# A two-layer metaformer on one Trainium2 core: image columns turned during the softmax, per-batch token scales, a pinned first norm

## The chip, the cores and the metric

The kernel runs on one core of a Trainium2 chip. The metric is the device time of one execution in microseconds (us); three executions are given by their median. Beside them stands one profiled execution, in which the hardware recorded every instruction of each engine. The engines are TensorE (PE in the profile; its weight loads are PEld), VectorE (DVE), ScalarE (ACT) and GpSimd (POOL); SyncE (SP) starts transfers. Each engine works through its own list of instructions and waits on semaphores for what others produce. On-chip data lies in SBUF (128 partitions) or, for results of TensorE, in PSUM.

## What is computed

The input is 4 batches of 32 images ("tokens") of 128 x 128 values. Layer 0 normalises each image row, runs an attention over tokens whose keys, queries and values come from Fourier convolutions, adds a mixer, and then a recurrent layer (FFN); layer 1 is an up/down convolution and a second FFN. The change touches the attention alone:

```python
tokens_norm = instance_norm(tokens, norm1_g, norm1_b)
k = fno_layer(tokens_norm, key_w, key_skip_w, key_skip_b, (Hs, Ws))
q = fno_layer(tokens_norm, query_w, query_skip_w, query_skip_b, (Hs, Ws))
v = fno_layer(tokens_norm, value_w, value_skip_w, value_skip_b, (H, W))
...
dprod = jax.nn.softmax(jnp.einsum('bhtd,bhsd->bhts', qf, kf) / scale, axis=-1)
attn = jnp.einsum('bhts,bhsd->bhtd', dprod, vf)
attn = fno_layer(attn, proj_w, proj_skip_w, proj_skip_b, (H, W))
attn = instance_norm(attn + tokens, attn_norm_g, attn_norm_b)
```

`x` reaches this part after a row norm: `x + _L0_conv_ref(_ln_c(x), ...)`. A convolution in `fno_layer` is a sum of a Fourier part over few frequencies and of a skip, a multiple of the image itself. So a score of head h between tokens t and s is a sum of a spectral product and of a multiple of the inner product ("gram") of the two images. The instance norm of a token is a factor s(t) on its image, and a score carries s(t) s(s).

## The kernel before

All images stay in SBUF as `XA[row, batch, token, column]`. The attention works in this order.

*Head.* `load` brings the images in eight rows of eight tokens for two batches first, with two loads of constants between them on SyncE's queue: L513 the first part, L519 the second (`cst[:, C_SW:]`). `stats(k, n)` (L737) takes for half batch k (16 images) the row statistics (`bn_stats`, one per image), a reciprocal root through `rsqrt_of` (L293 to L302: add, ACT root, reciprocal, four VectorE operations with a Newton step) and the factors r and nmr; `normalise(k, images)` (L759) applies them, 10 of 16 images on ScalarE (L765) and 6 on VectorE (L767). Two halves' statistics are written down first.

*Transforms.* The loop at L883 runs `transform(k)` over eight half batches: 16 images against 130 Fourier columns in groups of three (`ps_st1`, L782), copies to `A1` (L784 VectorE, L786 ScalarE), then the second Fourier dimension into `ps_pf` (L793) and the reduced images into `ps_pr` (L802), which ScalarE copies to `Rn` (L804). Between the groups, generators of other work are stepped: the statistics of the next batch, the weights' preparation (`weights`, which holds `ndcm`, L632), and `scores(b)` of the batch before.

*Scores* (L807). The coefficients `Frep` of a batch are gathered (`ps_fr`, L818), copied to `FK` (L825), multiplied with the query and key weights into `KM` (L832 to L847), transposed through `ps_kt` (L854), copied to `KT` by ScalarE (L855), and multiplied into the score tile `psc` (L858). `grams(k)` (L864) forms the inner products of the images of two batches from `Rn`.

*Softmax* (L899 to L967). After the loop the four scales `s4` come from `ps_s4`; the last batch's scores and the second grams follow. `Pm` is weight x gram + psc, times `sTL` (the product of the two tokens' scales), then max, subtraction, exponential, sum, reciprocal. The attention matrix is transposed (`ps_pt`, L949) and copied to `PTs` (L950) and its negative (L952); a weighted sum over heads gives `C`, which is transposed and spread over the blocks of `CTbd` (L967).

*Mixing.* `mix()` (L977) applies `CTbd` to all images at once. A chunk k is four image columns: four transposes bring (batch, token) to the partitions (`pt`, L982), ScalarE copies to `uT` (L984), four products give `pm` (L987), ScalarE copies them back to `XA` (L989) and squares them (L991, L994), and VectorE sums the squares (L995). Twenty of the chunks are interleaved with the Fourier part of the projection: 32 `df` products on VectorE (L1222) and bursts of `ps_y` on TensorE (L1235), one `mix` step after two or three of each four `df`.

The source order is not the order of execution. A scheduler places instructions by priorities from the source order and by their dependencies, on each engine apart, except where `in_order()` (L433) chains the instructions of each engine in a block to source order. Pools decide when buffers come free: `psa` holds two PSUM tiles (tag `st1`), `psb` three that `big(...)` hands out, and the mixing's PSUM pool `psm` takes over that space when these end.

Of the kernel before, what the change touches and what calls it, by code (L numbers as in the profile page):

```python
# [26 lines left out]
F32 = mybir.dt.float32  # L27
AF = mybir.ActivationFunctionType
ALU = mybir.AluOpType
# [3 lines left out]
P = 128  # L33
NB, NT = 4, 32
# [174 lines left out]
def _network(  # L209
# [53 lines left out]
    def scalar(name):  # L263
        o = len(HEAD_VECTORS) * NH + SCALARS.index(name)
        return sc[:, o : o + 1]
# [5 lines left out]
    def per_head(v):  # L271
        return v.unsqueeze(2).broadcast_to([P, NH, NT])
# [205 lines left out]
    PTs = WXY[:, 11072:12096].rearrange("p (a b c) -> p a b c", b=4, c=P)  # L478
    gram = aw.tile([P, NT], F32, name="gram")
# [15 lines left out]
    def big(name):  # L495
        return psb.tile([P, 512], F32, tag="big", name=name)
# [233 lines left out]
    with (  # L730
# [38 lines left out]
        def transform(k):  # L769
# [6 lines left out]
            normalise(k, range(0, 3))  # L776
            for n, j in enumerate(range(0, HB, 3)):
                m = min(3, HB - j)
                normalise(k, range(j + 3, min(j + 6, HB)))
                p = psa.tile([P, 3, 130], F32, tag="st1", name="ps_st1")  # L780
                for i in range(m):
                    mm(p[:, i, :], XA[:, b, t0 + j + i, :], cst[:, C_E : C_E + 130], start=True, stop=True)  # L782
                if n % 3 == 0:
                    nc.vector.tensor_copy(A1[:, j : j + m, :], p[:, :m])  # L784
                else:
                    nc.scalar.copy(A1[:, j : j + m, :], p[:, :m])  # L786
                yield True
# [19 lines left out]
        def scores(b):  # L807

            FF = sp.tile([P, 2, 16, NT], F32, tag="KM", name="FF")
# [4 lines left out]
            for g in range(4):  # L814
# [6 lines left out]
                if g % 2 == 1:  # L821
# [3 lines left out]
            nc.vector.tensor_copy(FK.rearrange("p r (k j w) -> p r k j w", k=8, j=2),  # L825
                                  Frep[:, b, :, :, 1:3, :WQ].rearrange("p k r j w -> p r k j w"))
# [49 lines left out]
        for k in range(2):  # L876
            for _ in stats(k, 1):
                pass
            if k == 0:
                next(prepare)  # L880
# [28 lines left out]
        for _ in before:  # L909
            pass  # L910

# [23 lines left out]
        Pm = sp.tile([P, NH, NT], F32, tag="KM", name="Pm")  # L935
        tt(Pm, per_head(wqk), per_token(gram), ALU.mult)
        tt(Pm, Pm, psc, ALU.add)
        tt(Pm, Pm, per_token(sTL), ALU.mult)
# [6 lines left out]
        tt(Pm, Pm, per_head(mx), ALU.mult)  # L945

        p = big("ps_pt").rearrange("p (g n) -> p g n", g=4)
        for g in range(4):
            nc.tensor.transpose(p[:, g], Pm[:, 4 * g : 4 * g + 4, :].rearrange("p h s -> p (h s)"), ident)  # L949
        tt(PTs[:, 0].rearrange("p g (b t) -> p g b t", b=NB), p.rearrange("p g (b t) -> p g b t", b=NB),  # L950
           s4.unsqueeze(1).unsqueeze(3).broadcast_to([P, 4, NB, NT]), ALU.mult)
        nc.scalar.mul(PTs[:, 1], PTs[:, 0], -1.0)  # L952

# [3 lines left out]
        Pv = sp.tile([P, NH, NT], F32, tag="KT", name="Pv")  # L957
        tt(Pv, Pm, per_head(pv_), ALU.mult)
        C = sp.tile([P, NT], F32, name="C")
        nc.vector.tensor_reduce(C, Pv.rearrange("p h s -> p s h"), AX.X, ALU.add)  # L960
        CT = sp.tile([P, NT], F32, name="CT")
        tt(C, C, sL, ALU.mult)
        tt(C, C, cst[:, C_ID : C_ID + 32], ALU.add)
        nc.vector.transpose(CT, C)
        for b in range(NB):
            q = slice(32 * b, 32 * b + 32)
            nc.vector.tensor_copy(CTbd[q, 32 * b : 32 * b + 32], CT[q])  # L967
# [9 lines left out]
    def mix():  # L977

        for k, w0 in enumerate(range(0, 80, 4)):
            pt = psm.tile([P, 4, P], F32, tag="pt", name="pt")  # L980
            for i in range(4):
                nc.tensor.transpose(pt[:, i, :], XA[:, :, :, w0 + i].rearrange("p b t -> p (b t)"), ident)  # L982
            uT = mp.tile([P, 4, P], F32, name="uT")
            nc.scalar.copy(uT, pt)  # L984
            pm = psm.tile([P, 4, P], F32, name="pm")
            for i in range(4):
                mm(pm[:, i, :], uT[:, i, :], CTbd, start=True, stop=True)  # L987
# [1208 lines left out]
```

## Time and profile before

| | us |
|---|---|
| median of three runs | 1044.66 |
| lowest and highest | 1043.44 and 1045.15 |
| profiled execution | 1045.66 |
| its span, first to last instruction | 1043.9 |

The mean granted clock of TensorE was 0.954 of full speed. Places in time are given from the start of the span. Operations that the change touches, in the profiled execution:

| operation | start, us | duration, us |
|---|---|---|
| first image norm on ScalarE, L765 | 17.80 | 3.19 for 8 |
| second constants load issued, L519 | 9.1 | 3.12 for the issue |
| `rep4` from those constants, POOL L524 | 16.8 | 0.32 |
| `FK` copy, batch 0, L825 | 43.23 | 0.31 |
| first `ps_kt` transposes, batch 0, L854 | 47.77 | 0.60 for 4 |
| `ps_s4` products, L901 | 112.53 | 1.05 for 4 |
| `psc` of the last batch, last four records, L858 | 123.81 | 1.90 |
| table load and first exponential, L912 | 123.34 | 1.28 |
| exponential of the scores, L942 | 128.80 | 0.63 |
| first `uT` copy, L984 | 134.83 | 0.59 |
| first `pm` products, L987 | 135.48 | 3.78 for two chunks |

How to read the lines below: a group names line, engine, operation, the tile written and the tile read, the shape and a count; TensorE's count of f32 products is two for each. In a timeline the bracket gives the engine's idle time before the group and the instruction that ended it. A chain of waits lists start, length and what ran, each piece released by the one before. The granted clock is the share of full speed that TensorE had.

### The profile page before, as it was taken

What the parts mean: (1) busy time and instruction counts of PE and PEld (TensorE: products, weight loads), DVE (VectorE), ACT (ScalarE), POOL (GpSimd) and SP (SyncE); (2) the same over time, 40 slices, a digit from 0 to 9 for tenths busy, and PEclk for the clock granted to TensorE, in tenths of its full rate; (3) what the DMA queues carried; (4) which work ended last, traced back from release to release, by engine and by line L of the source; (5) the groups of instructions that cost most, each with busy time, mean ns of one, the idle gap of its engine ahead of it and who ended that gap; (6) DMA issues with size and microseconds to landing.
All of it is one profiled execution on the core that took longest, in us unless ns stands there. A gap on an engine that the chain in (4) does not pass through costs nothing.

```text
span 1043.9 us, 18132 instructions
## 1 busy us (share of the span) xinstructions
PE 944.6 (90%) x6424; PEld 682.9 (65%) x6424; DVE 774.3 (74%) x2501; ACT 666.3 (64%) x1606; POOL 173.1 (17%) x298
## 2 busy tenths in 40 slices
PE   3999799977888999887998999999999999998995
PEld 2565466774655556534885777777777777776884
DVE  5986487775699998988888566665666666466997
ACT  3757356765567997967884545564656565556874
POOL 1000000021454436441001111102020202000000
PEclk9999989978789998999998999999999999999998
DMA  9723000001011110200000001000000000104543
GB/s 235 175 37 75 1 1 1 1 1 42 21 42 43 41 49 15 81 21 1 1 1 1 21 21 31 21 21 21 22 21 21 21 21 22 30 21 156 219 163 134
DMA packets 68965, 48.83 MB, mean 47 GB/s; under 512 B 4417, under 2 KB 63809, under 8 KB 68801
## 3 DMA queue, kind: packets, MB, share of 16 engines
q1 hardware_dynamic: 68529, 47.31, 15.7%
q8 instruction: 53, 0.87, 0.4%
q0 software_dynamic: 288, 0.01, 0.2%
q10 hardware_dynamic: 48, 0.26, 0.1%
q14 instruction: 47, 0.39, 0.1%
HBM read 30.68 MB, written 16.88 MB: 46 GB/s over the span
## 4 chain that ended last, share of the span: by engine, by line
PE 47%; DVE 24%; ACT 9%; POOL 6%; issue 3%; POOLq 0%; ACTq 0%; DVEq 0%
PE ps_scan L1841 8%; PE ps_up L1984 7%; PE ps_dn L1996 6%; PE ps_dn L2005 3%; PE ps_up L1973 3%; DVE XA L1511 3%; PE ps_wx L378 3%; PE ps_y L1235 2%; DVE XA L1510 2%; POOL c_r L292 2%; PE pm L987 2%; DVE U L1987 2%; POOL f_r L292 2%; PE ps_st L1353 2%; PE ps_inv L413 2%
## 5 line engine op out<-in xcount | busy, mean ns | idle before, releaser
L1987 DVE SCALAR_TENSOR_TENSOR U<-ps_up,above 128x512 f32<-128x512 f32 x128 | 86.7, 690 | 89.1 <-ACT above L1986 89.1
L1984 PE MATMUL ps_up<-q,WXY 128*128 128x512 f32 x256 | 123.6, 605 | 6.5 <-ACT q L1976 6.5
L1996 PEld LDWEIGHTS ps_dn<-WXY,U 128*128 128x128 f32 x1024 | 124.4, 192 | 3.3
L1996 PE MATMUL ps_dn<-WXY,U 128*128 128x128 f32 x1024 | 124.6, 275 | 0.0
L1842 DVE SCALAR_TENSOR_TENSOR ps_scan<-WXY,bs,ps_scan 128x128 f32<-128x128 f32 x352 | 103.6, 359 | 10.2 <-PE ps_scan L1841 7.3
L1986 ACT ACTIVATE above<-ps_up 128x512 f32<-128x512 f32 x128 | 74.3, 596 | 25.2 <-PE ps_up L1984 25.2
L1998 ACT COPY q<-ps_dn 128x512 f32<-128x512 f32 x64 | 37.5, 586 | 71.8 <-PE ps_dn L1996 71.8
L378 PE MATMUL ps_wx<-xt,wvt 128*128 128x512 f32 x128 | 68.8, 623 | 6.4 <-ACT WXY L385 4.2
L1973 PEld LDWEIGHTS ps_up<-WXY,XN 128*128 128x128 f32 x256 | 49.2, 192 | 34.5 <-issue 15.6
L292 POOL TENSOR_TENSOR f_r<-rs_e,neg_half 128x16 f32<-128x16 f32 (+2 forms) x10 | 23.9, 2394 | 278.6 <-DVE rs_e L291 244.1
L1984 PEld LDWEIGHTS ps_up<-q,WXY 128*128 128x128 f32 x256 | 44.0, 193 | 39.6 <-issue 23.9
L1973 PE MATMUL ps_up<-WXY,XN 128*128 128x256 f32 x256 | 66.8, 384 | 0.5 <-DVE XN L1943 0.5
L2005 PE MATMUL ps_dn<-q,WXY 128*128 128x256 f32 x256 | 66.0, 380 | 0.0
L1347 ACT ACTIVATE Z<-Z,k,aB 128x128 f32<-128x128 f32 x128 | 51.2, 482 | 11.7 <-DVE Z L1342 11.6
L2005 PEld LDWEIGHTS ps_dn<-q,WXY 128*128 128x128 f32 x256 | 46.1, 190 | 16.4 <-issue 12.0
L782 PE MATMUL ps_st<-cst,XA 128*128 128x130 f32 x256 | 43.3, 308 | 14.4 <-ACT XA L765 11.2
L385 ACT COPY WXY<-ps_wx 128x512 f32<-128x512 f32 x60 | 34.9, 582 | 28.6 <-DVE bn L381 28.4
L782 PEld LDWEIGHTS ps_st<-cst,XA 128*128 128x128 f32 x256 | 35.0, 204 | 27.5 <-ACT XA L765 12.4
L1568 ACT ACTIVATE xn<-XA,f_o,f_r 128x128 f32<-128x128 f32 x120 | 50.4, 487 | 2.7 <-DVE f_o L1550 2.2
L1945 ACT ACTIVATE XN<-XA,c_o,c_r 128x128 f32<-128x128 f32 x64 | 28.8, 490 | 31.8 <-DVE c_o L1934 25.9
L1511 DVE SCALAR_TENSOR_TENSOR XA<-Z,gB,XA 128x128 f32<-128x128 f32 x128 | 45.5, 355 | 4.7
L1510 DVE SCALAR_TENSOR_TENSOR XA<-ps_inv,r1B,xin 128x128 f32<-128x128 f32 x128 | 44.0, 344 | 6.4 <-PE ps_inv L1503 6.4
(436 smaller groups left out, 2147.4 us busy)
## 6 DMA issues: line engine op xcount, KB each, us to landing
XA<-in_x_dram SPq DMA_DIRECT2D x16, 512.0 KB, 7.3
xin<-in_x_dram SPq DMA_DIRECT2D x32, 256.0 KB, 3.2
turned<-XA SPq DMA_DIRECT2D x32, 256.0 KB, 2.3
XA<-turned SPq DMA_DIRECT2D x8, 1024.0 KB, 15.1
out_dram<-res SPq DMA_DIRECT2D x64, 128.0 KB, 2.1
WXY<-dd SPq DMA_DIRECT2D x4, 544.0 KB, 10.7
WXY<-md SPq DMA_DIRECT2D x4, 144.0 KB, 5.2
WXY<-m1d SPq DMA_DIRECT2D x1, 544.0 KB, 11.3
```

Source lines behind the costliest of these rows:

```text
L292: nc.gpsimd.tensor_tensor(o, e, neg_half[:, :n], ALU.pow)
L378: mm(self.held[t], self.t[:, 0, :], xt, start=True, stop=True)
L782: mm(p[:, i, :], XA[:, b, t0 + j + i, :], cst[:, C_E : C_E + 130], start=True, stop=True)
L1511: stt(a, Z[c][:, b, i], gB[c][:, n : n + 1], a, ALU.mult, ALU.add)
L1841: mm(p4, self.t[:, 1, :], prev, start=True, stop=True)
L1842: stt(p4, WX[:, :, h, :], s[:, 0:1], p4, ALU.mult, ALU.add)
L1973: mm(p[:, b, :], XN[u // 2][:, (u % 2) * H2 + b, :], UR.rearrange("p r q -> p (r q)"), start=True, stop=True)
L1984: mm(p, UC[:, s, :], q, start=True, stop=True)
L1986: nc.scalar.activation(above, p, AF.Relu, scale=1.0 - SLOPE)
L1987: stt(U[:, s], p, SLOPE, above, ALU.mult, ALU.add)
L1996: mm(p[:, r, b, :], U[:, s, b, r * P : (r + 1) * P], DC[:, s, :], start=(s == 0), stop=(s == 1))
L2005: mm(p, DR[:, r, :], q[:, r], start=(r == 0), stop=(r == 1))
```

## The change

Five things are done.

1. In the head the row statistics of half batch 0, the norm of all its 16 images and the statistics of half batch 1 are chained in this order by `in_order()`. `transform(0)` no longer norms.
2. The scale `s4` of a batch is computed at the start of its `scores(b)`. `FK` is multiplied by it on the way (two multiplies in place of one copy), so keys and queries both carry their own batch's scale. The gram part gets its scales by multiplying `gram` (128 x 32) with `sTL`, and the multiplication of `Pm` (128 x 512) goes.
3. `turn_images` transposes the columns of the first eight mixing chunks into `psa` tiles (`st1`, widened to 512 values) and ScalarE copies them to `turned_images`, a region of `WXY`. Four chunks stand in the source after the first product of `Pm`, four after the exponential.
4. `mix()` takes these eight chunks as they are and transposes only from chunk 8 on.
5. After the softmax's reciprocal a chained block computes `C` and `CTbd` first, from unnormalised `Pm` with the reciprocal in `pv_`, and then normalises, transposes and copies `PTs`.

```diff
@@ -476,6 +476,7 @@
+    turned_images = WXY[:, 12288:16384].rearrange("p (k i n) -> p k i n", k=8, i=4)
@@ -773,11 +774,13 @@
-            normalise(k, range(0, 3))
+            if k > 0:
+                normalise(k, range(0, 3))
             for n, j in enumerate(range(0, HB, 3)):
                 m = min(3, HB - j)
-                normalise(k, range(j + 3, min(j + 6, HB)))
-                p = psa.tile([P, 3, 130], F32, tag="st1", name="ps_st1")
+                if k > 0:
+                    normalise(k, range(j + 3, min(j + 6, HB)))
+                p = psa.tile([P, 512], F32, tag="st1", name="ps_st1")[:, : 3 * 130].rearrange("p (m n) -> p m n", m=3)
@@ -806,6 +809,12 @@
         def scores(b):
+            p = big("ps_s4")[:, :1]
+            mm(p, rv4[:, b].rearrange("p q t -> p (q t)"), mean_mat[:, 0:1], start=True, stop=True)
+            nc.vector.tensor_copy(s4[:, b : b + 1], p)
+            rsqrt_of(a1p, s4[:, b : b + 1], s4[:, b : b + 1], 1e-5, 1)
+            ts(s4[:, b : b + 1], s4[:, b : b + 1], scalar("norm1_g"), None, ALU.mult)
@@ -822,8 +831,9 @@
-            nc.vector.tensor_copy(FK.rearrange("p r (k j w) -> p r k j w", k=8, j=2),
-                                  Frep[:, b, :, :, 1:3, :WQ].rearrange("p k r j w -> p r k j w"))
+            for r in range(2):
+                ts(FK[:, r].rearrange("p (k j w) -> p k j w", k=8, j=2), Frep[:, b, :, r, 1:3, :WQ], s4[:, b : b + 1],
+                   None, ALU.mult)
@@ -873,11 +883,13 @@
-        for k in range(2):
-            for _ in stats(k, 1):
+        next(prepare)
+        with in_order():
+            for _ in stats(0, 1):
                 pass
-            if k == 0:
-                next(prepare)
+            normalise(0, range(HB))
+            for _ in stats(1, 1):
+                pass
@@ -894,20 +906,21 @@
-        p = big("ps_s4")[:, :NB]
-        for b in range(NB):
-            mm(p[:, b : b + 1], rv4[:, b].rearrange("p q t -> p (q t)"), mean_mat[:, 0:1], start=True, stop=True)
-        nc.vector.tensor_copy(s4, p)
-        rsqrt_of(a1p, s4, s4, 1e-5, NB)
-        ts(s4, s4, scalar("norm1_g"), None, ALU.mult)
         for _ in range(5):
             next(before)
         for _ in grams(1):
             pass
         for _ in before:
             pass
+        def turn_images(chunks):
+            for k in chunks:
+                p = psa.tile([P, 512], F32, tag="st1", name="ps_pt").rearrange("p (i n) -> p i n", i=4)
+                for i in range(4):
+                    nc.tensor.transpose(p[:, i, :], XA[:, :, :, 4 * k + i].rearrange("p b t -> p (b t)"), ident)
+                nc.scalar.copy(turned_images[:, k], p)
@@ -933,38 +946,41 @@
+        tt(gram, gram, sTL, ALU.mult)
         tt(Pm, per_head(wqk), per_token(gram), ALU.mult)
+        turn_images(range(0, 4))
         tt(Pm, Pm, psc, ALU.add)
-        tt(Pm, Pm, per_token(sTL), ALU.mult)
...
         nc.scalar.activation(Pm, Pm, AF.Exp)
+        turn_images(range(4, 8))
         nc.vector.tensor_reduce(mx, Pm, AX.X, ALU.add)
         nc.vector.reciprocal(mx, mx)
-        tt(Pm, Pm, per_head(mx), ALU.mult)
-
-        p = big("ps_pt").rearrange("p (g n) -> p g n", g=4)
...
-        tt(Pv, Pm, per_head(pv_), ALU.mult)
...
+        with in_order():
+            Pv = sp.tile([P, NH, NT], F32, tag="KT", name="Pv")
+            tt(pv_, pv_, mx, ALU.mult)
+            tt(Pv, Pm, per_head(pv_), ALU.mult)
+            C = sp.tile([P, NT], F32, name="C")
+            nc.vector.tensor_reduce(C, Pv.rearrange("p h s -> p s h"), AX.X, ALU.add)
...
+            for b in range(NB):
+                q = slice(32 * b, 32 * b + 32)
+                nc.vector.tensor_copy(CTbd[q, 32 * b : 32 * b + 32], CT[q])
+            tt(Pm, Pm, per_head(mx), ALU.mult)
+
+            p = big("ps_pt").rearrange("p (g n) -> p g n", g=4)
+            for g in range(4):
+                nc.tensor.transpose(p[:, g], Pm[:, 4 * g : 4 * g + 4, :].rearrange("p h s -> p (h s)"), ident)
...
+            nc.scalar.mul(PTs[:, 1], PTs[:, 0], -1.0)
@@ -977,11 +993,14 @@
         for k, w0 in enumerate(range(0, 80, 4)):
-            pt = psm.tile([P, 4, P], F32, tag="pt", name="pt")
...
+            if k < 8:
+                uT = turned_images[:, k]
+            else:
+                pt = psm.tile([P, 4, P], F32, tag="pt", name="pt")
...
```

More of the change, by code (lines that the diff above doesn't have):

```diff
@@ L942, in _network @@
         nc.scalar.activation(Pm, Pm, AF.Exp)
+        turn_images(range(4, 8))
         nc.vector.tensor_reduce(mx, Pm, AX.X, ALU.add)
         nc.vector.reciprocal(mx, mx)
-        tt(Pm, Pm, per_head(mx), ALU.mult)
-        p = big("ps_pt").rearrange("p (g n) -> p g n", g=4)
[L948 to L951, printed above, removed]
@@ L952, in _network @@
-        nc.scalar.mul(PTs[:, 1], PTs[:, 0], -1.0)
         pv_ = sp.tile([P, NH], F32, name="pv_")
         tt(pv_, head("proj_skip_w"), head("value_skip_w"), ALU.mult)
[L957 to L967, printed above, removed]
+        with in_order():
[4 more added lines that the diff above has]
+            nc.vector.tensor_reduce(C, Pv.rearrange("p h s -> p s h"), AX.X, ALU.add)
+            CT = sp.tile([P, NT], F32, name="CT")
+            tt(C, C, sL, ALU.mult)
+            tt(C, C, cst[:, C_ID : C_ID + 32], ALU.add)
+            nc.vector.transpose(CT, C)
+            for b in range(NB):
[5 more added lines that the diff above has]
+                nc.tensor.transpose(p[:, g], Pm[:, 4 * g : 4 * g + 4, :].rearrange("p h s -> p (h s)"), ident)
+            tt(PTs[:, 0].rearrange("p g (b t) -> p g b t", b=NB), p.rearrange("p g (b t) -> p g b t", b=NB),
+               s4.unsqueeze(1).unsqueeze(3).broadcast_to([P, 4, NB, NT]), ALU.mult)
+            nc.scalar.mul(PTs[:, 1], PTs[:, 0], -1.0)
@@ L979, in mix @@
         for k, w0 in enumerate(range(0, 80, 4)):
-            pt = psm.tile([P, 4, P], F32, tag="pt", name="pt")
[L981 to L984, printed above, removed]
+            if k < 8:
+                uT = turned_images[:, k]
+            else:
+                pt = psm.tile([P, 4, P], F32, tag="pt", name="pt")
+                for i in range(4):
+                    nc.tensor.transpose(pt[:, i, :], XA[:, :, :, w0 + i].rearrange("p b t -> p (b t)"), ident)
+                uT = mp.tile([P, 4, P], F32, name="uT")
+                nc.scalar.copy(uT, pt)
             pm = psm.tile([P, 4, P], F32, name="pm")
```

## The prediction

> **What bounds the kernel now.** I read the page first: busy shares (part 1) and the chain that ended last (part 4). TensorE is busy for 90% of the span and carries most of the chain, so time saved elsewhere counts only where TensorE waits for it.
>
> ```profile
> PE 944.6 (90%) x6424; PEld 682.9 (65%) x6424; DVE 774.3 (74%) x2501; ACT 666.3 (64%) x1606; POOL 173.1 (17%) x298
> ...
> PE 47%; DVE 24%; ACT 9%; POOL 6%; issue 3%; POOLq 0%; ACTq 0%; DVEq 0%
> ```
>
> All edits act before 205 us. I cut that stretch with the table of windows (us, then busy time and instruction count of PE, PEld, DVE, ACT, POOL, then granted clock, DMA share and GB/s): head, first scores, transforms, softmax, mixing.
>
> ```profile
> 0.00:48.00 48.00, 28.40 (x194) 20.26 (x195) 36.08 (x182) 26.06 (x67) 5.10 (x16) 1.00 0.95 222
> 48.00:63.00 15.00, 14.73 (x104) 8.23 (x102) 13.14 (x63) 9.35 (x23) 0.00 (x0) 1.00 0.02 6
> 63.00:113.00 50.00, 48.25 (x359) 29.72 (x357) 32.82 (x145) 30.11 (x72) 1.72 (x3) 1.00 0.29 57
> 113.00:133.50 20.50, 13.64 (x105) 9.58 (x104) 13.90 (x31) 6.79 (x17) 0.90 (x1) 0.81 0.00 1
> 133.50:204.20 70.70, 69.77 (x542) 46.95 (x542) 53.34 (x63) 45.58 (x72) 0.00 (x0) 0.96 0.00 1
> ```
>
> Mixing is TensorE's (69.8 of 70.7 us busy); the softmax is a chain with TensorE idle for 6.9 of 20.5 us. The head (DMA share 0.95) waits for data. The chain of waits through the softmax (start, us, what):
>
> ```profile
> 115.49 5.34 PE pg L868 x64
> 121.09 1.48 PE ps_kt L854 x12
> ...
> 123.88 1.85 PE psc L858 x4
> 125.75 0.69 DVE Pm L937
> 126.62 0.70 DVE Pm L938
> ...
> 130.47 0.70 DVE Pm L945
> 131.20 0.70 DVE Pv L958
> 131.92 1.01 DVE C L960
> 132.93 0.61 DVE WXY L950
> 133.59 2.00 PE pt L982 x8
> 135.59 3.67 PE pm L987 x16
> ```
>
> The timeline shows that TensorE's idle time is there, and which engine makes the head wait (duration, then idle before and releaser in brackets):
>
> ```profile
> 131.31 1.08 PE L949 MATMUL ps_pt<-ident,Pm 128*128 128x128 f32 x4 [5.59 <-DVE Pm L945]
> ```
>
> ```profile
> 121.77 1.56 ACT L855 COPY KT<-ps_kt 96x512 f32<-96x512 f32 x3
> ```
>
> [...] the three KT copies stand in one unbroken row in program order; so what the program now puts ahead of them delays them. [...] mean granted clock 0.54 from 130 to 140 us after the idle from 125.7, and two pm chunks (x16) take 3.67 us there where they take 2.2 us (2 x 1.10) later. [...]
>
> **The change, part by part.** The order in which the built program issues instructions on each engine, set against before's, decides here.
>
> *Head.* The first half batch's 16 norms now stand ahead of the 16 bn_stats of the second. In before VectorE waits for those images for 3.45 us (10.65 to 14.10) with the first rsqrt chain still unfinished behind them, and the first ACT norm starts at 17.80. That wait goes. But in the new order VectorE has ndcm (L632) ahead of the rest of the rsqrt chain; it reads the second constants load (L519), in before it ran at 57.52. The only reader that shows when that load lands is POOL's L524, which waits 11.5 us for it and starts at 16.8. So the chain resumes at 16.8; L301, L302 and L749 with small operations between take about 0.8, and the first norm is at about 17.6: 0.2 gained. The bn_stats (16 x 0.29 = 4.6 us, 11 of them in before done while waiting) come afterwards; I walk the second half batch's pf to 36.5, 35.72 in before. Head: +0.8; bounds −5 (norms at 12.5, if the load lands early) and +1.5.
>
> *The tokens' scale inside the scores.* Per batch one ps_s product, a copy, five small VectorE operations, one ACT root and a multiply, 7 x about 0.12 + 0.2 of ACT = 1 us with the handovers; once for four batches before. FK becomes two multiplies of about 0.25 for one copy of 0.31. The multiply by norm1_g, and FK with all behind it, moves in batch 0 behind the filter preparation on VectorE. KM is then ready near 56.3, in before its transposes ran at 47.77. TensorE's new order has pf and stage 1 of half batch 3 first, reaches kt(0) near 53.6, and waits about 2.8. With the ps_s products, pr(3) ends 3.1 later than 63.15. Later TensorE has idle slots in before (0.36 at 87.3, 0.22 and 0.57 before 98, 0.44 at 109.66, 50 − 48.25 = 1.75 in that window) that take part of it. Lag at the end of pr(7), 112.53 in before: +2, bounds +0.5 to +3.5. If the idle slots do not absorb, it stays 3.1.
>
> *Softmax, counted from P, the end of pr(7).* In before: grams P+2.9 to P+8.2, kt P+8.5 (121.0), psc ends P+13.2 (125.73), first mixing product P+22.95 (135.48). After: one ps_s instead of four (0.25 for 0.98) lets grams end at P+7.25. But 30 of the 32 image transposes (chunks 0 to 6 and half of 7) stand ahead of kt in TensorE's queue, and seven of their copies ahead of the KT copies in ACT's. With two PSUM buffers a chunk waits for the copy of the last but one, so seven copies of 0.57 (mean of KT and uT copies, 0.55 to 0.60) = 4.0 us set the pace: kt at P+12.0, psc ends P+16.9, 3.7 late. The cover for these copies, the idle softmax, lies after psc and only the eighth lands there. Then L937, max, subtract, Exp, sum and reciprocal take 3.85, against 4.7 in before, as Pm x sTL (0.70) left the 512-wide path: P+20.75. Now Pv 0.72 (+0.15 pv_), C 0.97, C twice and CT 0.67, CTbd 4 x 0.19 = 0.75, all ahead of Pm x recip 0.70, four transposes about 1.0 (cold) and PTs 0.68: sum 5.85 with handovers, first mixing product at P+26.6. It waits for the PTs copy since its PSUM is what ps_pt held. In before the transposes lay beside Pv and C. Difference 26.6 − 22.95 = +3.65. df (L1222, the other head of mixing) starts there too, P+22.4 in before, +4.2.
>
> *Mixing.* In before the pt transposes of chunks 0 and 1 ended before the first pm. So of eight chunks' transposes only six still go: 6 x 0.58 = 3.5 on a TensorE that is full, plus 0.1 to 0.5 where pm had waited for uT (0.48 at 147.4). The eight uT copies (8 x 0.59) leave ACT, which is not the bound. VectorE per group has 4 df of 1.25 and 2.5 squares of 0.69 = 6.7 us per 8.4 us group, so nothing takes TensorE's place. −3.7, bounds −5 (all eight chunks) and −2.5 (ACT's pm copies and squares, 1.73 per chunk, pace the first four).
>
> *Clock.* TensorE idles from about P+16.9 to P+24.7, so the first products are cold again, as now; +0 to +1 if the half clock reaches further. I take +0.3. Exp tables: one load of 1.28 in both.
>
> *DMA order.* m1d goes before dd on SP; dd is first read by df near 139, both were landed long before: 0.
>
> Sum: 2.0 + 3.65 − 3.7 + 0.3 = +2.25, of which the head is already inside the lag of 2. I take +2.5. The profiled execution was 1045.66 with a span of 1043.9 (1.8 around it) and lies 1.0 above the median of 1044.66; 1045.66 + 2.5 = 1048.2 in its terms, 1047.2 in terms of the median, which is forecast. A measurement of this kernel can tell about 0.2%, 2.1 us, from no change.
>
> **Rivals.**
> A, *faster*: the turning does what its place in the source says. If the KT copies are not held by image copies (ACT catches up during the grams, 5 us in which it idles: 4.95 before L925), psc ends at P+12.25, the reciprocal at P+16.1 and the first product comes 5.85 later, at P+21.95: tail −1.0; with −3.7 for mixing, a lag of 0.5 and 0.3 of clock −3.9, near 1040.8. For it: ACT's idle. Against it: the order puts the image transposes after the grams on TensorE's queue. Chance 0.19.
> B, *about the same*: tail and mixing cancel (+3.65 − 3.7), and the stall at kt(0) is taken up by the slots before 110, or the head gains the 3.45 wait because the constants landed earlier: +0.3, 1045. Chance 0.22.
> C, *slower, my forecast*: +2.5, 1047.2. Chance 0.42.
> D, *clearly slower*: lag 3.3 stays, tail +4.2 by df, mixing only −2.5 as ACT paces the first chunks, and a cold start of 1: +6, 1050.7. One mechanism decides, the copies in ACT's queue: beyond 0.57 x 7 each further 0.1 us per copy is 0.7 on the path. Chance 0.17.
> E, *the change does not do what it says*: the norms are pinned but start no sooner (part of C's head), no case of its own.
>
> **How the numbers follow.** Faster by over 0.2% (below 1042.6): A's 0.19 less a little that lies above, plus a little of B: 0.2. Within (to 1046.75): most of B and the low edge of C: 0.24. Slower: C's rest and D, 0.56. Range 1041 to 1051: it leaves out over half of A (0.11) and the end of D (0.06). The likeliest case's own range is 1045.5 to 1049.
>
> **What would show it.** Right: POOL's L524 and ndcm beside each other near 16.8 and the first norm just after; a TensorE wait of about 3 us before kt(0); an unbroken row of seven image copies on ACT ahead of KT; psc ending about 17 after pr(7); no pt transposes before chunk 8 and mixing about 67 us long. Wrong: the first norm near 12.5; KT copies in among the image copies; a mixing stage that shrinks by more than 5, or by less than 2 because ACT or df sets its pace.

## The result, and the profile after

The changed kernel takes 1057.77 us (median of four runs, 1055.52 to 1060.5); the kernel before takes 1044.91 beside it. It is 12.9 us slower by the medians and 12.2 by the ratio, 1.0117 with a 95% interval of 1.0104 to 1.013. The forecast was 2.5 slower, and 1051 was the upper end of its range.

The profiled execution has a span of 1056.0 us against 1043.9, at a mean granted clock of 0.955 against 0.954. That mean leaves out the head: the first record of the granted clock in the trace lies at 36.1 us (26.5 before), and what is ahead of it counts as full clock. From these records on, TensorE spends 97.0 us at half clock, 97.8 before; so outside the head the 12.1 us are not a matter of clock as a whole.

In what follows pf is the second Fourier product (`ps_pf`), and pr 0 to pr 7 are the eight reduced products (`ps_pr`), one for each half batch. The table of windows of the changed kernel is cut at events (us, then busy time and count of PE, PEld, DVE, ACT, POOL, granted clock, DMA share, GB/s). The second window ends where the fourth reduced product (pr 3) ends, the third with the last one (pr 7), the fourth where the first mixing product starts, the fifth with the last ps_y burst:

```profile
0.00:48.00 48.00, 27.02 (x151) 17.98 (x152) 31.06 (x173) 20.37 (x51) 5.08 (x16) 1.00 0.97 222
48.00:73.40 25.40, 21.68 (x146) 12.39 (x145) 22.76 (x99) 16.73 (x42) 0.00 (x0) 0.93 0.04 1
73.40:122.80 49.40, 47.87 (x361) 29.97 (x361) 31.74 (x141) 29.17 (x70) 1.72 (x3) 1.00 0.27 59
122.80:149.70 26.90, 17.55 (x131) 12.99 (x131) 15.10 (x41) 11.65 (x26) 0.90 (x1) 0.85 0.00 1
149.70:216.20 66.50, 65.07 (x512) 42.77 (x512) 51.88 (x55) 41.34 (x66) 0.00 (x0) 0.96 0.00 1
```

The kernel before, cut at the same events:

```profile
48.00:63.20 15.20, 14.93 (x105) 8.29 (x103) 13.34 (x63) 9.55 (x23) 0.00 (x0) 1.00 0.02 6
63.20:112.60 49.40, 47.65 (x355) 29.27 (x353) 32.59 (x145) 29.55 (x71) 1.72 (x3) 1.00 0.30 58
112.60:135.50 22.90, 15.96 (x116) 11.62 (x116) 15.75 (x39) 8.40 (x19) 0.90 (x1) 0.78 0.01 1
135.50:204.20 68.70, 67.85 (x535) 45.31 (x534) 51.52 (x55) 44.32 (x70) 0.00 (x0) 0.97 0.00 1
```

What counts is where the events stand. The fourth reduced product ends at 73.4 (63.2 before, +10.2), the last at 122.8 (112.6, still +10.2), the first mixing product starts at 149.7 (135.5, +14.3), the last ps_y burst ends at 216.2 (204.2, +12.0). After that nothing more is lost: the remaining 839.8 us are 839.7 before. So most of the loss is in the first 74 us, and the stretch from 73.4 to 122.8 takes up nothing of it.

*The head.* TensorE's timeline of the changed kernel, then of the kernel before (start, duration):

```profile
30.15 0.80 PE L785 MATMUL ps_st<-cst,XA 128*128 128x130 f32 x2 [1.19 <-ACT XA L766]
30.89 1.94 PE L796 MATMUL ps_pf<-A,cst 128*32 128x256 f32 x16
32.75 3.57 PE L805 MATMUL ps_pr<-A,cst 128*64 128x512 f32 x8
...
41.64 1.07 PE L796 MATMUL ps_pf<-A,cst 128*32 128x256 f32 x16 [0.36 <-ACT A L789]
```

```profile
28.16 1.07 PE L793 MATMUL ps_pf<-A,cst 128*32 128x256 f32 x16
29.16 1.94 PE L802 MATMUL ps_pr<-A,cst 128*64 128x512 f32 x8
...
35.72 1.07 PE L793 MATMUL ps_pf<-A,cst 128*32 128x256 f32 x16 [0.35 <-ACT A L786]
```

The first pf group runs at 30.89 and takes 1.94, where the second takes 1.07, and the reduced product takes 3.57 instead of 1.94: by these lengths TensorE is at half clock here, where the trace has no clock record yet. In the kernel before both groups take 1.07. Ahead of the first pf stands the first image of the second half batch, and TensorE waits 1.19 us for its norm. Why that norm is late is in the timelines of VectorE and ScalarE:

```profile
17.09 0.15 DVE L633 TENSOR_SCALAR ndcm<-cst 128x1 f32<-128x1 f32 x1 [4.96 <-DMA cst<-in_consts_dram]
```

```profile
27.63 0.48 ACT L789 COPY A<-ps_st 128x390 f32<-128x390 f32 x1 [3.06 <-PE ps_st L785]
28.01 0.22 ACT L298 ACTIVATE rq_q<-rq_e 128x16 f32<-128x16 f32 x1
29.01 0.27 ACT L789 COPY A<-ps_st 128x130 f32<-128x130 f32 x1 [0.77 <-PE ps_st L785]
29.61 3.95 ACT L766 ACTIVATE XA<-XA,p_n,p_r 128x128 f32<-128x128 f32 x10 [0.33 <-DVE p_n L750]
```

VectorE stands 4.96 us before one tiny operation, as foretold, and the first norm starts at 18.01. The second half batch's root (L298) stands on ScalarE behind a copy that waits 3.06 us for TensorE; its input had been ready at 25.3. The factors of that half are ready at 29.6, in the kernel before at 23.5 (L749, 23.29 and 0.16 long).

*The first scores.* TensorE's timeline of the changed kernel, then of the kernel before:

```profile
61.99 0.64 PE L864 MATMUL ps_kt<-ident,KM 128*96 128x128 f32 x4 [2.32 <-DVE KM L856]
62.56 2.90 PE L805 MATMUL ps_pr<-A,cst 128*64 128x512 f32 x8
65.39 1.75 PE L864 MATMUL ps_kt<-ident,KM 128*96 128x128 f32 x8
```

```profile
47.77 0.60 PE L854 MATMUL ps_kt<-ident,KM 128*96 128x128 f32 x4
48.30 1.94 PE L802 MATMUL ps_pr<-A,cst 128*64 128x512 f32 x8
```

The wait for KM is 2.32 us, where the kernel before has none, and what follows is slow as well: the reduced product takes 2.90 where it takes 1.94 elsewhere, eight transposes 1.75 where they take 1.08.

*The softmax.* The chain of waits of the changed kernel:

```profile
130.59 0.87 PE ps_pt L921 x4
131.46 0.02 issue
131.48 0.61 ACT WXY L922
132.09 0.04 issue
132.13 0.87 PE ps_pt L921 x4
133.00 0.02 issue
133.02 0.60 ACT WXY L922
...
134.84 1.31 PE ps_kt L864 x12
```

Image transposes and their copies alternate for 4.3 us, with all that releases the scores behind them. Further down the same chain, CTbd's copies and the multiply of Pm stand in line before the transposes that the first mixing product waits for:

```profile
146.75 0.18 DVE WXY L975
146.93 0.01 issue
146.94 0.70 DVE Pm L976
147.65 0.14 issue
147.78 1.10 PE ps_pt L980 x4
148.88 0.02 issue
148.91 0.70 DVE WXY L981
```

### The profile page after: what moved, and what is told of

Read it like the earlier page. It is cut to its first block, busy times and chain, and to the rows that moved or that the text cites. A ratio compares the mean times of both kernels' runs of the same rounds, so it can differ in the third digit from the quotient of the medians.

```text
span 1056.0 us, 18160 instructions
## 1 busy us (share of the span) xinstructions
PE 949.5 (90%) x6424; PEld 684.6 (65%) x6424; DVE 780.7 (74%) x2527; ACT 670.2 (63%) x1609; POOL 173.6 (16%) x298
## 4 chain that ended last, share of the span: by engine, by line
PE 58%; DVE 20%; ACT 11%; POOL 6%; issue 3%; DMA 1%; SPq 1%; POOLq 0%; ACTq 0%; DVEq 0%
PE ps_scan L1860 10%; PE ps_up L2003 8%; PE ps_dn L2015 7%; PE ps_dn L2024 3%; PE ps_up L1992 3%; PE ps_wx L378 3%; DVE XA L1530 3%; PE ps_st L785 3%; PE ps_inv L413 2%; PE ps_y L1254 2%; PE pm L1006 2%; DVE XA L1529 2%; POOL c_r L292 2%; ACT Z L1366 2%; DVE U L2006 2%
## 5 line engine op out<-in xcount | busy, mean ns | idle before, releaser
L385 ACT COPY WXY<-ps_wx 128x512 f32<-128x512 f32 x60 | 35.0, 583 | 27.1 <-DVE bn L381 25.7
L381 DVE BATCH_NORM_STATS2 bn<-ps_wx 128x6 f32<-128x512 f32 x64 | 44.1, 692 | 6.0 <-PE ps_wx L378 5.6
## 6 DMA issues: line engine op xcount, KB each, us to landing
XA<-turned SPq DMA_DIRECT2D x8, 1024.0 KB, 14.3
```

## The experiments

Each was timed beside the kernel before on the same chip, and the ratio is to that kernel, with its 95% interval. The row "changed" is from the four runs of the result; the changed kernel was not timed again beside its variants. The other columns come from one profiled execution of each: the end of the last reduced product (pr 7), the time from there to the end of the last psc, and from that to the end of the last ps_y burst. Such columns scatter by about a microsecond: in the nine kernels with the head of before, the second pf starts between 35.7 and 36.9.

| kernel | ratio | pr 7 ends | to psc | to ps_y |
|---|---|---|---|---|
| before | 1 | 112.6 | 13.1 | 78.5 |
| changed | 1.0117 (1.0104 to 1.013) | 122.8 | 16.9 | 76.5 |
| without_head | 1.0089 (1.0069 to 1.0109) | 119.3 | 16.9 | 76.2 |
| without_scale | 1.0066 (1.0047 to 1.0085) | 119.7 | 18.8 | 76.7 |
| without_turn | 1.0049 (1.0032 to 1.0065) | 121.7 | 11.9 | 77.2 |
| without_order | 1.0063 (1.0043 to 1.0083) | 121.0 | 16.9 | 74.0 |
| alone_head | 1.0058 (1.0039 to 1.0078) | 117.9 | 12.1 | 78.3 |
| alone_scale | 1.0054 (1.0037 to 1.0071) | 118.8 | 11.9 | 76.6 |
| alone_turn | 1.003 (1.0016 to 1.0043) | 114.2 | 17.2 | 75.1 |
| alone_order | 1.0013 (1.0003 to 1.0024) | 113.5 | 13.2 | 78.2 |
| turn_idle | 0.9934 (0.9915 to 0.9953) | 113.0 | 13.1 | 72.7 |
| scale_early | 0.9998 (0.999 to 1.0007) | 113.5 | 11.9 | 77.0 |
| head_free | 0.9996 (0.9986 to 1.0006) | 114.1 | 13.1 | 78.5 |
| idle_early | 0.995 (0.9937 to 0.9962) | 113.6 | 11.9 | 73.1 |
| after_early | 1.0079 (1.0056 to 1.0102) | 118.1 | 16.8 | 75.9 |
| after_ndcm | 1.0136 (1.0104 to 1.0168) | 114.9 | 16.9 | 76.1 |
| after_idle | 1.013 (1.0098 to 1.0162) | 121.4 | 11.9 | 76.2 |
| after_all3 | 1.0032 (1.0014 to 1.0049) | 115.6 | 11.9 | 76.0 |
| idle_early_head | 0.9987 (0.9974 to 0.9999) | 118.1 | 11.9 | 73.2 |
| idle_early_again | 0.9956 (0.9942 to 0.997) | 113.4 | 11.9 | 73.2 |

**One part undone.** The change was cut into head (pinned norms and statistics), scales (inside the scores, gram x sTL), turning (`turn_images`, chunks taken by `mix`) and order (the chained last part of the softmax). Each kernel below is the changed one with one part as it was before.

> The changed kernel with the head of the kernel before (statistics of both halves free, norms inside the transforms); the scales, the turning and the softmax order stay. Theory A (lags add): in the trace the second coefficients' product (L793) of half batch 2 ends 5.5 us later than before because of the head, and nothing later takes that up, so this run is 5.5 us faster than the changed kernel, about 1052.3. Rival B (the lags overlap: the first score transposes would wait for their scale chain anyway): under 2 us faster, 1056 or more.

Measured: about 2.9 us less than the changed kernel by the ratios. Rival B's side: the two lags overlap. With the head of before, the third coefficients' product is again at 46.8 (46.4 before), but the first kt transposes come no sooner than 59.1, as KM is computed behind the filter preparation whatever the head does. The wait grows by what the head gave up, and pr 7 ends only 3.5 us earlier.

> The changed kernel with the tokens' scales after the loop, as in the kernel before; head, turning and softmax order stay. Theory A (lags add): the 4.6 us lost between half batches 2 and 3 come back, the softmax gets 0.7 (512-wide multiply by sTL) and 0.7 (three more ps_s products) longer, so about 3.2 us faster than the changed kernel, 1054.6. Rival B (the wait for the first score transposes comes from the late head alone): within 1 us of the changed kernel.

Measured: 5.3 us less. pr 7 ends 3.1 earlier, and the softmax is 1.9 longer to psc, so the profiled execution (1056.64, the slowest of its six) shows only part of the gain. Neither theory's number; the scales matter, and a lag of 7.1 at pr 7 stays.

> The changed kernel with all chunks turned inside the mixing; head, scales and softmax order stay. Theory A (image copies stand ahead of the KT copies): the softmax is 3.7 us shorter, the mixing 2.3 longer as the trace has it, so about 1.4 us faster, 1056.4. Rival C (turning pays, the loss is elsewhere): 2 to 4 us slower than the changed kernel, 1060 or more.

Measured: 7.1 us less, against all that was expected. The way to psc is 5.0 us shorter, so the mechanism is there; but the mixing gives back only 0.7 (77.2 against 76.5), not 2.3 or 3.7. Turning hardly pays in this kernel.

> The changed kernel with the softmax's last part in the order of the kernel before (Pm times reciprocal first, transposes beside Pv and C). Theory A: CTbd's four copies and the pv product no longer stand ahead of Pm, 0.8 to 1.1 us faster, about 1056.8. Rival D (the order is most of the tail's 4.1 us): 3 us or more faster, 1054.8 or less.

Measured: 5.6 us less. The columns say where 2.5 of it are: from psc to the last ps_y burst 74.0 against 76.5. With the old order the turned chunks do pay: 74.0, where scale_early and alone_scale below, without turned chunks, have 77.0 and 76.6. The total is in rival D's range, but its reason, an order that is bad by itself, fails below: alone the order costs 1.4. The order takes away what the turning gains. It is seen in the starts after psc: in the changed kernel the first df product starts 9.9 us after it and the first mixing product 10.1, here both 8.3.

**One part alone** in the kernel before.

> The kernel before with only the head changed. From the changed kernel with its scales put back, where the third reduced product (L802) ended 6.4 us later than before: theory A, that lag reaches the end of the transforms with nothing taking it up, and the rest is as before: 5 to 7 us slower than before. Rival B (the lag is taken up by TensorE's idle slots before 113 us, 1.75 us of them): 3.5 us slower or less.

Measured: 1.0058, 6.1 us. Theory A; pr 7 ends 5.3 late, and pr 3 already did: nothing takes it up.

> The kernel before with only the tokens' scales moved into the scores. With the head of before the changed kernel still lost 7.7 us by the fourth reduced product. Theory A: the first scores wait for a multiply that stands in VectorE's list behind the filter preparation, +7; the softmax gets back 1.4 to 2: about 5 us slower than before. Rival B (the wait arises only together with the late or the turned parts): within 2 us of before.

Measured: 1.0054, 5.6 us. Theory A. The cause is in VectorE's timeline of this kernel (start, duration, line, tiles):

```profile
53.49 0.66 DVE L538 TENSOR_TENSOR WXY<-WXY,hp 32x496 f32<-32x496 f32 x1
...
54.43 0.20 DVE L813 TENSOR_SCALAR s<-s,sc 128x1 f32<-128x1 f32 x1
...
55.14 0.48 DVE L831 TENSOR_SCALAR FK<-WXY,s 128x144 f32<-128x144 f32 x2
```

The multiply by norm1_g reads `sc`, and that load is issued late, at 39.9 in the changed kernel and 40.6 in without_head. The built program has the multiply behind operations of the filter preparation (hp), and with it FK and KM. It does not wait for the data: in these two kernels the load lands 6.3 and 6.0 us after its issue, at 46.2 and 46.6, 11.2 and 8.0 us before the multiply runs (57.40 and 54.56), and VectorE's timelines before the multiply (from 40 us in without_head, 44 in the changed kernel, 48 here) show no wait for a load. What holds it is its place in VectorE's list.

> The kernel before with only the turning of eight chunks. Theory A: seven image copies stand ahead of the KT copies, psc ends 3.7 to 4.9 us later; the mixing gives back 3.8: 0 to 1 us slower than before. Rival C (turning as such is bad, also in the mixing): 3 us slower or more.

Measured: 1.003, 3.1 us. Rival C's number, just, with an interval of 1.7 to 4.5 us, but theory A's mechanism. In the profile the way to psc is 4.1 longer and that to the last ps_y 3.4 shorter, about what theory A has; pr 7 stands 1.6 late, 1.2 of it already at the first pf, where nothing is changed. Where the remaining 1 to 2 us of the median are was not settled.

> The kernel before with only the last part of the softmax in the new order. Theory A: the first mixing product waits for the PTs copy behind C and CTbd, 0.8 us later, and df too, 1.5 later: 1 to 1.5 us slower than before. Rival D (the new order is good without the turned chunks, as the mixing's own transposes wait for nothing of it; the run without turning showed a short mixing): 1 us or more faster than before.

Measured: 1.0013, 1.4 us. Theory A's number; the columns show almost nothing (78.2 against 78.5). The first mixing product starts 4.1 later after psc than before, but the stage from there to the last ps_y is 4.3 shorter (the first two chunks' products take 2.34 where they took 3.78; the rest was not traced).

**The place of the copies.** The turning alone, its work chained behind what it had stood in front of:

```diff
         for _ in grams(1):
             pass
-        for _ in before:
-            pass
+        with in_order():
+            for _ in before:
+                pass
+            turn_images(range(0, 4))
...
-        nc.scalar.activation(Pm, Pm, AF.Exp)
+        with in_order():
+            nc.scalar.activation(Pm, Pm, AF.Exp)
+            turn_images(range(4, 8))
```

> The kernel before with only the turning, and its transposes chained behind the last psc product on TensorE, its copies behind the KT copies and, for the last four chunks, behind the exponential on ScalarE. Theory A (only the place of the copies costs): psc ends where it did before, the mixing gives 3 to 4 back: 3 to 4 us faster than before, near 1041. Rival C (turning as such gains nothing, the mixing is paced by something else): within 1 us of before.

Measured: 0.9934, 6.9 us faster than before, more than expected, 10 us faster than the same work in the other place. ScalarE's and TensorE's timelines of this kernel:

```profile
122.17 1.56 ACT L856 COPY KT<-ps_kt 96x512 f32<-96x512 f32 x3
...
126.93 1.19 ACT L916 COPY WXY<-ps_pt 128x512 f32<-128x512 f32 x2 [1.69 <-PE ps_pt L915]
```

```profile
126.04 4.54 PE L915 MATMUL ps_pt<-ident,XA 128*128 128x128 f32 x24
130.74 1.44 PE L915 MATMUL ps_pt<-ident,XA 128*128 128x128 f32 x8 [0.15 <-ACT WXY L916]
132.02 0.66 PE L962 MATMUL ps_pt<-ident,Pm 128*128 128x128 f32 x4
...
135.95 2.05 PE L1003 MATMUL pm<-WXY 128*128 128x128 f32 x16
```

KT goes first, the turning fills the 5.59 us in which TensorE was idle, and the clock stays up (1.00 from 122 to 132 us): the transposes of Pm take 0.66 instead of 1.08, the first two mixing chunks 2.05 instead of 3.78. From psc to the last ps_y 72.7, 5.8 less than before.

**The scalars' load.** Scales alone, the load moved:

```diff
     nc.sync.dma_start(cst[:, C_SW:], consts[:, C_SW:])
+    nc.sync.dma_start(sc, scal.partition_broadcast(P))
...
-        nc.sync.dma_start(sc, scal.partition_broadcast(P))
         nc.sync.dma_start(fw, ffn)
```

> The kernel before with only the tokens' scales in the scores, and the load of the scalars (sc, which holds norm1_g) issued right after the second constants instead of as the last but one of the preparation's loads. In the built order the multiply by norm1_g, FK and KM then stand ahead of the filter preparation again, and TensorE's first kt transposes ahead of the fourth pf. Theory A (the late load of the scalars placed the whole first score chain late): the 5.6 us of the scales alone go, and the shorter softmax is left: 1 to 2 us faster than before. Rival E (the longer chain of small operations itself costs): 3 to 6 us slower than before.

Measured: 0.9998. The 5.6 us are gone, which shows the place of the load in the program to be the cause, by way of the built order: the multiply now runs at 41.71 and kt at 48.1. The 1 to 2 us that the shorter softmax was to leave do not show in the time (to psc 1.2 less and to ps_y 1.5 less, pr 7 0.9 later).

**The constants' wait.** Head alone, `ndcm` chained behind `hermitian` so that it cannot stand in front:

```diff
-        ts(ndcm, dcm, -1.0, 1.0, ALU.mult, ALU.add)
-        hermitian(m12[:, 0, 0], m12[:, 0, 1], wp.tile([P, KH - 1], F32, tag="hm", name="hm"), dcm)
+        with in_order():
+            hermitian(m12[:, 0, 0], m12[:, 0, 1], wp.tile([P, KH - 1], F32, tag="hm", name="hm"), dcm)
+            ts(ndcm, dcm, -1.0, 1.0, ALU.mult, ALU.add)
```

> The kernel before with only the head changed, and ndcm chained behind the first operations on the filter weights, so that nothing of the second constants load stands ahead of the rsqrt chain. Theory A (two causes: the wait for the constants, and the second half's statistics behind all norms): norms start near 12.5 and pf(0) near 24, the second half's norms no later than in before; the loss of 6.1 goes and the time is within 1.5 us of before, as the next batches' images set the pace. Rival F (the chained order itself, statistics behind norms, is the loss): still 3 us or more slower than before.

Measured: 0.9996, theory A. The norms start at 12.87, 5 us earlier, and the loss is gone. But nothing is won: the first pf is at 25.7 (28.2 before), at half clock (1.94), and the second at 36.6 (35.7).

> The kernel before with the turning in the softmax's idle time and the scales in the scores with the scalars loaded early. Theory A: both gains add, 7 to 9 us faster than before and 1 to 2 faster than the turning in idle time alone. Rival G (the gains overlap in the softmax): no faster than the turning in idle time alone, 6 to 7 us faster than before.

Measured: 0.995, and 0.9956 in the repeat, 5.2 and 4.6 us. Rival G: no faster than the turning in the idle time alone, and a little less than the 6 to 7 it said.

**Mending the changed kernel** in one of the three places, then in all.

> The changed kernel with only the load of the scalars issued early, so that the first scores' chain stands ahead of the filter preparation. Theory A (the late scalars cost what the scales cost inside the whole): 4 to 6 us faster than the changed kernel, ratio to before about 1.007. Rival B (the late head makes the scores wait anyhow): under 2 us faster, ratio 1.010 or more.

Measured: 1.0079, some 4 us faster: theory A at its lower edge, with an interval that reaches rival B's 1.010. In the trace the wait for KM and the half clock behind it are gone (reduced product 1.94).

> The changed kernel with only ndcm put behind the filter weights, so that the first norms do not wait for the second constants. Theory A (the wait is the head's whole loss, and overlaps the late scalars as the head did): 3 us faster than the changed kernel, ratio to before about 1.009. Rival H (full 6 us come back): ratio about 1.006.

Measured: 1.0136, no gain in the median, where the profiled execution ended pr 7 7.9 us earlier and took 1049.69. Four others of this kernel took 1058.45 to 1059.54, at granted clocks of 0.944 to 0.946 against 0.953, and a sixth, which the ratio leaves out, 1068.54 at 0.932. What differs in them was not seen; this run decides nothing about the time.

> The changed kernel with only the turning chained behind psc and the KT copies. Theory A (the place of the copies costs some 4 us in the softmax and 2 to 3 in the mixing): 7 to 9 us faster than the changed kernel, ratio to before about 1.004. Rival D (in the new softmax order the turned chunks wait for PTs and only the softmax's 4 come back): 4 to 5 us faster, ratio about 1.0075.

Measured: 1.013, no gain in the median, at a mean clock of 0.944. In its profile psc comes 5.0 us sooner after pr 7 (11.9), so the copies no longer stand ahead; to the last ps_y it still takes 76.2. What follows is on rival D's side for the profile, and open for the time. As the changed kernel was not timed on that chip beside these two, it is open too whether its own clock would have been lower there.

> The changed kernel with all three mended: scalars early, ndcm late, turning in the idle time; the pinned norms, the scales in the scores and the softmax order of the change stay. Theory A (these three placements are the whole loss): 4 to 6 us faster than before, ratio 0.994 to 0.996. Rival I (something else of the change costs too, such as the pinned statistics or the order): ratio 0.998 or more.

Measured: 1.0032: most of the loss gone, but rival I. Two things are left. One is the order: from psc to the last ps_y 76.0, and 75.9 to 76.7 in every kernel with the new order and turned chunks. The other is in VectorE's timeline of this kernel:

```profile
17.37 0.18 DVE L947 TENSOR_TENSOR wqk<-sc 128x16 f32<-128x16 f32 x1 [4.71 <-DMA sc<-in_scal_dram]
17.55 0.17 DVE L751 SCALAR_TENSOR_TENSOR p_n<-p_m,p_r 128x16 f32<-128x16 f32 x1
```

With the scalars loaded early, another tiny operation (wqk) moved in front of the norms and waits 4.71 us for that load. So the start of the norms was not mended here (17.76 against 18.01); only the instruction at its front changed.

> The mended kernel (scalars early, ndcm late, turning in the idle time, norms pinned) with the softmax's last part in the order of the kernel before. Theory A (with chunks turned ahead, the new order holds the first mixing product back and costs 2.9 us from psc to the last ps_y burst; the pinned head costs the other 3): ratio to before 0.999 to 1.001. Rival J (the order costs nothing, the pinned head is everything): ratio 1.002 to 1.004, as with all three mended.

> The kernel before with scales in the scores, scalars early and turning in the idle time, once more on this chip. Theory A: 3 us faster than the kernel with the pinned head beside it, ratio to before 0.994 to 0.996. Rival J: about 6 us faster than the one beside it with a like ratio of 0.995. Rival D (the order is everything, the pinned head costs nothing): as the one beside it.

Measured side by side: 0.9987 and 0.9956. The pinned head, again held by wqk (5.00 us), costs 0.3%: theory A. That the wait for wqk is its cause was not tested by moving wqk. The new order costs about 0.45% (1.0032 to 0.9987, on two chips); of these 4.7 us the columns show 2.8 (76.0 against 73.2).

**The clock.** Every run lists its granted clock. Over 331 runs (the one at 0.932 left out), a line fitted with a level of its own for each kernel, and for before in each group, gives 0.54 us for 0.001 of clock. At one clock of 0.956 before lies at 1045.4 to 1046.7, the changed kernel at 1056.7, alone_head at 1051.1, alone_scale at 1050.4, alone_turn at 1048.5, turn_idle at 1043.6, after_early, after_ndcm and after_idle at 1052.1 to 1053.0. So by the fit each of the three mendings gains about 4 us, and two of them lost it again at a lower clock in that group; why it was lower is open. These are fits, not measurements of one kernel, over means that leave out the head. They also take from a kernel what it gains by keeping the clock up: turn_idle, 6.9 us faster as measured, keeps 3.1 of that (1043.6 against 1046.7 for before in its group).

## Why the prediction was wrong

**The sign and the mechanisms that it named** were right: slower; VectorE waits before ndcm until 17.09 (16.8 said); TensorE waits for the first KM by 2.32 (2.8 said); psc ends 16.9 after pr 7 (16.9 said); the first mixing product 27.0 after it (26.6 said). That work put ahead of the KT copies delays them was read from one row of three; alone_turn (17.2 to psc) beside turn_idle (13.1), with the same eight chunks, shows it.

Two of these sizes agree in part by luck. Both ends of the wait for KM came some 6 us later than the walk had them: TensorE was ready at 59.7 (53.6 said), KM at 61.9 (56.3 said). And of the way to psc, the grams end 6.4 after pr 7 (7.25 said; the prediction's own terms, 8.2 less 0.73, give 7.5), while the image transposes then hold kt back for 5.5 us where 4.75 was said.

**The step that failed is the lag at the end of pr 7**: "+2, bounds +0.5 to +3.5" was 10.2. Three terms made it.

*The head, +0.8 said, +5.9 measured* (pf of the second half batch at 41.6, 36.5 said). The walk is given by its end alone, and names neither of two things that the trace shows. The root of the second half stood behind a ScalarE copy until 28.01, so that the first pf waited for an image of that half. And by the lengths of its products TensorE ran at half clock until about 36, where the clock records begin, and in the kernel before until about 26.5 (eight stage-1 records take 2.10 at 20.34 and 1.16 at 97.19). How much is clock: after_all3 starts its norms at nearly the same time (17.76 against 18.01), but has six stage-1 records in 0.94 us where the changed kernel needs 1.67; its pf groups are at 28.3 and 38.1. So up to 3.5 us of the 5.9 are, by this estimate, the longer half clock. The other 2.4 are not the order alone, as after_all3 too is at half clock in its first pf (1.94) and much of its first reduced product (2.59). The changed kernel's execution is also the latest of its kind: in the six other kernels whose first norms are held by ndcm, the second pf starts between 39.9 and 40.9.

*The first scores, +2.3 said, +4.7 measured* (the lag grows from 5.5 at the third pf to 10.2 at the fourth reduced product). Of this 2.3 is the wait, and 1.7 the half clock behind it: the reduced product (2.90 for 1.94) and the transposes (1.75 and 0.64 for 1.08 and 0.60). The prediction had looked for half clock after the softmax only. The step was mis-sized by more than that, because a late head hides part of it: with the head of before (alone_scale, without_head) KM is ready at 59.0 and 59.1 where 56.3 was said, and the same stretch loses 7.3 and 7.4.

*The taking-up, −1.1 said, 0 measured.* From the fourth to the last reduced product both kernels take 49.4 us, and alone_head too. Most idle slots of that stretch end with copies of stage 1, that is with waits inside the loop itself, which would move along with a late start; that this is the reason was not tested. And it is not a rule: in alone_scale 1.3 us, in without_head 1.0 us of the lag at pr 3 were gone at pr 7.

**The mixing, −3.7 said, −2.2 measured** (66.5 for 68.7 from the first product; as the new order moves that start, the times from psc say more). The count of transposes was right for the old order: with it the turned chunks gain 3.0 to 3.9 (77.0 to 74.0, or 73.1 in idle time). The new order withholds 2.5 to 2.9 of that: PTs come last, and df and the first product start 1.6 and 1.8 us later after psc. The rest of the 2.5 was not traced. The prediction priced the order as a matter of the softmax only.

**The rivals.** A, the faster one, was right that the turning pays in the right place, and wrong that the built program had it there. That turn_idle came out at 1040.7, where A had 1040.8, is chance: A's sum is for all five parts, and before stood at 1047.0 in that group. D, "clearly slower", came nearest: a lag that stays, +4.2 to the first df and −2.5 for the mixing are about what was measured, but it had the lag at 3.3. The range's upper end took the half clock as at most 1 us and the head as at most 1.5.

How the parts share the 12.9 us stays partly open: alone they cost 6.1, 5.6, 3.1 and 1.4 us, sum 16.2; undone they give back 2.9, 5.3, 7.1 and 5.6. Head and scales overlap at the first scores, and turning and order cost more together than apart.

## What to carry to other kernels

Read in the built order what stands ahead of the work you bring forward and what it waits for: a tiny operation on a late load (ndcm, then wqk) stood ahead of the first norms here, and the multiply by norm1_g stood behind other work though its data had landed; mending ndcm and the load of the scalars brought wqk to the front. Work that is moved into idle time has to be chained behind the work that ends before the idle time; in front of it, the same eight chunks cost 3 us, behind it they gained 7. An idle slot inside a loop may be no reserve where its cause is the loop itself: here the changed kernel made up none of its 10.2 us over four half batches.

## What was not expected of the hardware

A short wait was followed here by a loss beyond itself. In the changed kernel the clock records show half clock (0.50) from 63.4 to 66.8 us, just after the wait of 2.32 us for KM, which is less than half of the 5.59 us for which TensorE stands idle in the softmax of the kernel before, where the clock is 0.54 from 130 to 140 us. Slow products follow that wait in alone_scale too (3.07 us, then a reduced product of 3.10) and in without_head (3.06, then 3.28); scale_early and after_early, without the wait, have 1.94. It is not the only way there: in without_scale a pf group takes 1.83 at 51.20 (1.07 elsewhere) and the kt transposes behind it 1.06 for 0.60, with no wait above 0.57 from 44 to 57 us. What length of wait it takes was not shown.

The head of the changed kernel, with waits of 0.57 to 1.19 us from 22 to 31 us, stayed at half clock until 36 us. Its window reads 1.00 all the same, as the trace has no clock record before 36.1; the half clock is read from the durations (pf 1.94 for 1.07). That the waits are the cause was not tested.

Runs of the kernel before differ by 6 us with their mean granted clock (1045 at 0.959, 1051 at 0.948), so a gain of less than that needs many runs, or a comparison at equal clock.
